# A bidirectional recurrence with a sign-weight product: eight products moved to earlier steps, the last row groups in another order

## The chip, the cores and the metric

One core of one Trainium2 chip runs the whole program. The metric is device time in microseconds of one execution; three runs of the kernel before gave 488.4, 488.56 and 490.11 us, a median of 488.56. One further execution was taken by the hardware profiler.

## The reference, cut to what matters

With B = 4 batches, T = 1024 positions and C = 1024 channels:

```
decay = exp(-exp(w)) * (0.5 + 0.5 * tf)           # per batch and channel
ek, ekv = exp(k), exp(k) * k                       # k is also v
nf, nb = scan of ekv over t, forward and backward  # a = a * decay + ekv_t
df, db = scan of ek  over t, forward and backward
num = nf + nb - ekv + exp(u + k) * k
den = df + db - ek  + exp(u + k)
y = sigmoid(x) * num / max(den, 1e-8) * (0.8 + 0.2 * tf)
bw = sign(weight) * mean(|weight|) per output row
out = x + y @ bw.T + bias
```

## The kernel before

The recurrence runs over 32 blocks of 128 channels, block g = 8 * batch + cc, each a tile of 128 channels by 1024 positions. The loop `for g in range(steps)` makes one step for each; all engines' orders are written out by hand in it (`tc.manual_schedule()`), so an instruction waits behind whatever stands ahead of it on its engine.

In one step TensorE turns the rows of k for block g + 1 into `kT` (L272, `pe_transpose_k`) and the rows of sigmoid(x) for block g into `sgT` (L278, `pe_transpose_gate`). There is one buffer of each in PSUM: `kT` may be written again when VectorE has made `euk` from it (L362), and `sgT` when VectorE has read it in `dve_newton_gate` (L429). VectorE runs the four scans (L372 forward, L385 backward; the backward ones start from a value that ScalarE makes, L378, `edge_num` and `edge_den`) and three or four further operations. ScalarE makes the exponentials (L284, L290), the logarithm (L410) and the reciprocal (L417), and casts the finished block to a high part (L439, `act_hi`); GpSimd multiplies and makes the low part (L444, `lo_part`). So each finished block stands in `gated` as two parts, and each product with a block is two matmuls.

The product with the signs of the weight is spread over later steps. For the first three batches it comes in groups q of 128 output channels by 512 positions, 16 groups a batch: `pe_product` (L455) adds eight blocks into a PSUM tile of the pool `ps_o`, which has three buffers; `act_scale` (L467) scales it to `z`; `pe_turn` (L475) turns `z` back to rows; `act_leave` (L565) copies it to a staged tile, and every second group is stored. `parts[g][0..4]` lists what step g issues at its five places: place 0 ahead of `kT`, place 1 behind it, place 2 ahead of `sgT`, places 3 and 4 behind it. In the kernel before, groups 37 to 47 (the last eleven of the third batch) fill places of four blocks each from step 26 on, and end with places 0 and 1 of step 30. The queues `fresh`, `ready`, `scaled` and `leaving` hold groups that are done, can be scaled, can be turned, and can leave.

The last batch has its product the other way round, with rows of positions as the output: row groups n = 0 to 7 of 128 positions, in two halves (part 0 and 1) of 512 columns, 16 matmuls each (`pe_wide_product`, L523). Rows 6 (`begun`) have five of eight blocks done early as `partial` tiles (`pe_partial`, in step 30), which ScalarE copies out (L560). Some of the wide tiles are begun in steps 30 and 31 with the blocks that are ready. The tiles of rows 3 take the buffer of `sgT`; so that it is free, ScalarE copies the gate of the last block to `gate_of_last` (L821). Behind the loop, VectorE finishes block 31 in two halves, TensorE adds blocks 30 and 31 to rows 0 to 3, and then makes rows 4, 5, 7 and the rest of rows 6. VectorE scales each half by `alpha_rows` (L540), adds it to rows of x + bias (L542), and SP stores the rows (L839, `store_rows`).

Of the kernel before, what the change touches and what calls it, by code (L numbers as in the profile page):

```python
# [9 lines left out]
F32 = mybir.dt.float32  # L10
# [11 lines left out]
def kernel(  # L22
# [27 lines left out]
    nc = tc.nc  # L50
    P = 128
    B, T, C = x.shape
    TD = time_emb.shape[1]
    NT = T // P
    NC = C // P
# [13 lines left out]
    num_pool = ctx.enter_context(tc.tile_pool(name="num_pool", bufs=3))  # L69
# [4 lines left out]
    ps_o = ctx.enter_context(tc.tile_pool(name="ps_o", bufs=3, space=bass.MemoryType.PSUM))  # L74
# [6 lines left out]
    sg_ps = {}  # L81
# [437 lines left out]
    def pe_wide_columns(t, n, cols, blocks, ends=(0, NC - 1)):  # L519
        h, s = divmod(n, PER)  # L520
        for cc in blocks:
            for i in range(2):
                nc.tensor.matmul(  # L523
                    t,
                    gated[last, cc, h][:, i, s * P : (s + 1) * P],
                    wT[:, cc, cols],
                    start=(cc == ends[0] and i == 0),
                    stop=(cc == ends[1] and i == 1),
                )
# [6 lines left out]
    def columns(part):  # L536
        return slice(part * H, (part + 1) * H)

    def leave_columns(ps, n, cols):
        nc.vector.tensor_mul(ps, ps, alpha_rows[:, cols])  # L540
        xs = x_rows[n][:, cols]
        nc.vector.tensor_add(xs, xs, ps)  # L542
# [5 lines left out]
    begun = NT - 2  # L548
# [3 lines left out]
    def pe_partial(part):  # L552
        t = ps_o.tile([P, H], F32, tag="po", name=f"partial_{part}")
        pe_wide_columns(t, begun, columns(part), range(NC - 3), (0, NC - 4))
        partial_ps[part] = t
# [13 lines left out]
    steps = B * NC  # L569
# [6 lines left out]
    parts = {g: [[] for _ in range(5)] for g in range(steps)}  # L576
    late = {g: [] for g in range(steps)}
    groups = NH * NC

    def pieces(qs):  # L580
        return [(q, part) for q in qs for part in (front, back)]

    def fill(g, part, items):
        for i, piece in enumerate(items):
            ahead, at = divmod(part + i, 5)
            parts[g + ahead][at].append(piece)

    for g in range(lag, 2 * NC + 1):
        q = 2 * (g - lag)
# [13 lines left out]
        late[g + 1].append((q + i, range(NC - 1, NC)))  # L603
    for part, piece in enumerate(pieces((q + 3, q + 4))):
        parts[g + 1][1 + part].append(piece)
    fill(g + 2, 0, pieces(range(q + 5, q + groups)))


    adds = {g: [] for g in range(steps + 1)}
# [15 lines left out]
    g = 3 * NC  # L625
# [3 lines left out]
    with tc.manual_schedule():  # L629
# [39 lines left out]
        def done():  # L669
            while fresh:  # L670
                ready.append(fresh.pop(0))

        def scale():
            while ready:
                scaled.append(ready.pop(0))
                act_scale(scaled[-1])
# [6 lines left out]
        def leave():  # L683
            if leaving:
                act_leave(leaving.pop(0))

        for g in range(steps):
            b, cc = divmod(g, NC)
            final = g == steps - 1
            if g + 2 < steps:  # L690
                load_k(g + 2)
                for i in gate_loads[g]:
                    load_gate(i)
            else:
                load_x_rows(g + 2 - steps, rows, "k_rows")
                load_x_rows(g + 4 - steps, gate_rows, "sg_rows")
            if g < NC:
                load_weight(g)
            if g in begins:
                begin_rows(begins[g])  # L700
            if final:
                alpha_rows = load_along_rows(den_pool, "den", "alpha_rows", alpha_dram)

            if g > 0:
                dve_denominator(g - 1)
                dma_own_numerator(g - 1)
            for i in adds[g]:
                add_x(*i)
            if final:
                done()  # L710
            scale()
            if final:
                act_partial(1)
            done()
            if g > 1:
                act_hi(g - 2, 0)
                act_hi(g - 2, 1)
            product(parts[g][0])
            if final:
                pe_wide_product(1, 1, range(NC - 3))  # L720
                pe_wide_product(2, 0, range(NC - 3))
            turn()
            if g > 0:
                floor_den(g - 1)
            if g > 0 and not adds[g]:
                act_log(g - 1)
            pool_clamp(g)
            if g > 1:
                lo_part(g - 2, 0)
                lo_part(g - 2, 1)  # L730
            product(late[g][:2])
            if late[g]:
                done()
            if g > 0:
                forward(g, nums[g])
            act_edge(g, nums[g], "edge_num")
            if g > 0 and adds[g]:
                act_log(g - 1)
            if g > 0:
                act_reciprocal(g - 1)  # L740
                den_product(g - 1)
            if g > 0:
                dve_own_terms(g)
            scale()
            done()
            leave()
            if 1 <= g <= NC:
                prepare_weight(g - 1)
            if g == NC:
                out_scales()  # L750
            if not final:
                pe_transpose_k(g + 1)
                product(late[g][2:])
                act_exponentials(g + 1)
                act_own_exponentials(g + 1)
            scale()
            product(parts[g][1])
            turn()
            if final:
                for i in ((1, 0), (1, 1), (2, 0)):  # L760
                    pe_wide_product(*i, range(NC - 3, NC - 2))
                pe_wide_product(0, 0, range(NC - 2))
            backward(g, nums[g], "edge_num")
            if final:
                dma_own_numerator(g)
            if g > 0:
                num_product(g - 1)
            forward(g, dens[g])
            act_edge(g, dens[g], "edge_den")
            leave()  # L770
            done()
            scale()
            product(parts[g][2])
            if g == steps - 2:
                pe_partial(0)
            if g > 0:
                dve_newton_gate(g - 1)
            if g > 0 and not final:
                gated_product(g - 1)
            for i in gates[g]:  # L780
                act_gate(i)
            if gates[g]:
                log_exp_tables()
            pe_transpose_gate(g)
            if g == 3 * NC - 1:
                load_gate(g + 4)
            product(parts[g][3])
            turn()
            if g == steps - 2:
                leave()  # L790
                act_partial(0)
                pe_partial(1)
            if parts[g][4]:
                done()
            product(parts[g][4])
            if g == steps - 2:
                pe_wide_product(1, 0, range(NC - 3))
            leave()
            backward(g, dens[g], "edge_den")
            if not final:  # L800
                dve_numerator_terms(g + 1)
            if g == NC:
                store_alpha()
# [6 lines left out]
        for i in adds[steps]:  # L810
            add_x(*i)

        for ts in halves:
            dve_denominator(g, ts)
        for ts in halves:
# [1 line left out]
            act_log(g, ts)  # L817
        for ts in halves:
            act_reciprocal(g, ts)
        gate = num_pool.tile([P, T], F32, tag="num", name="gate_of_last")  # L820
        nc.scalar.copy(gate, sg_ps[g])  # L821
        sg_ps[g] = gate
        for i in ((0, 1), (2, 1), (3, 0), (3, 1)):
            pe_wide_product(*i, range(NC - 2))
        gated_product(g - 1, engine=nc.vector)
# [12 lines left out]
        def store_rows(n, cols=slice(0, C)):  # L838
            nc.sync.dma_start(  # L839
                out=out[last, n * P : (n + 1) * P, cols], in_=x_rows[n][:, cols]  # L840
            )
# [4 lines left out]
        for n, part in waiting:  # L846
            leave_wide(n, part)
            if part == 1:
                store_rows(n)
        for n, part in ((4, 0), (4, 1), (5, 0), (5, 1), (7, 0), (7, 1)):  # L850
            pe_wide_product(n, part, range(NC))

            for i in ((0, 1) if part else ()) if n == 5 else (part,):
                leave_wide(n, i)
            if (n, part) == (4, 1):
                nc.vector.tensor_mul(partials[0], partials[0], alpha_rows)
                nc.vector.tensor_add(x_rows[begun], x_rows[begun], partials[0])
            if part == 1 and n != 7:
                store_rows(n)
        store_rows(7)  # L860
        for cols in (slice(0, H), slice(H, 3 * H // 2), slice(3 * H // 2, C)):
            t = ps_o.tile([P, cols.stop - cols.start], F32, tag="po", name=f"rest_{cols.start}")
            pe_wide_columns(t, begun, cols, range(NC - 3, NC), (NC - 3, NC - 1))
            leave_columns(t, begun, cols)
            store_rows(begun, cols)


# [28 lines left out]
```

## Time and profile before

| what | value |
|---|---|
| median of three runs | 488.56 us (488.4 to 490.11) |
| the profiled execution's own time | 488.17 us |
| span of its instructions | 486.4 us |
| mean granted TensorE clock | 0.906 |
| busy: PE, DVE, ACT, POOL | 364.9, 468.9, 337.4, 406.2 us |
| first start of kT of block 31 on PE | 416.97 us |
| last VectorE instruction, start | 482.82 us |

The profile names TensorE PE (its weight loads PEld), VectorE DVE, ScalarE ACT, GpSimd POOL and SyncE SP. Times are microseconds from the span's start. A line of a timeline reads: start, length, engine, line of the kernel, operation, output and inputs, shape, count, and in brackets how long the engine stood idle before it and what ended that. The ends of matmuls are modelled; with pipelining, one may be issued before the modelled end of the last. PEclk is the granted clock as a share of full speed.

### The profile page before, as it was taken

What the parts mean: (1) busy time and instruction counts of PE and PEld (TensorE: products, weight loads), DVE (VectorE), ACT (ScalarE), POOL (GpSimd) and SP (SyncE); (2) the same over time, 40 slices, a digit from 0 to 9 for tenths busy, and PEclk for the clock granted to TensorE, in tenths of its full rate; (3) what the DMA queues carried; (4) which work ended last, traced back from release to release, by engine and by line L of the source; (5) the groups of instructions that cost most, each with busy time, mean ns of one, the idle gap of its engine ahead of it and who ended that gap; (6) DMA issues with size and microseconds to landing.
All of it is one profiled execution on the core that took longest, in us unless ns stands there. A gap on an engine that the chain in (4) does not pass through costs nothing.

```text
span 486.4 us, 5204 instructions
## 1 busy us (share of the span) xinstructions
PE 364.9 (75%) x1803; PEld 297.1 (61%) x1803; DVE 468.9 (96%) x325; ACT 337.4 (69%) x468; POOL 406.2 (84%) x280
## 2 busy tenths in 40 slices
PE   3444433344588777778899898965999998999996
PEld 2333332333466665566677777754887777888884
DVE  6999999999999999999999999999999999999864
ACT  4795968859576968859697968877867979734000
POOL 3379999999999999999999999999999999983000
PEclk9995566666699999999999999995999999999999
DMA  8877569896399595969877996979649797899963
GB/s 230 245 217 185 160 171 222 171 263 166 92 261 218 141 223 145 226 166 235 197 185 163 261 225 170 204 177 237 153 77 275 168 236 240 172 279 268 226 222 130
DMA packets 91282, 97.35 MB, mean 200 GB/s; under 512 B 2772, under 2 KB 80888, under 8 KB 89208
## 3 DMA queue, kind: packets, MB, share of 16 engines
q1 hardware_dynamic: 84264, 63.45, 44.0%
q0 software_dynamic: 6976, 33.57, 36.1%
q8 instruction: 14, 0.23, 0.2%
q14 instruction: 12, 0.10, 0.1%
q10 hardware_dynamic: 16, 0.00, 0.0%
HBM read 63.46 MB, written 37.75 MB: 208 GB/s over the span
## 4 chain that ended last, share of the span: by engine, by line
DVE 76%; PE 17%; issue 3%; ACT 3%; DMA 0%; SPq 0%; DVEq 0%; ACTq 0%
DVE den L385 13%; DVE num L385 13%; DVE num L372 13%; DVE den L372 12%; PE wide L523 9%; DVE den L395 7%; DVE num L356 6%; DVE den L429 6%; DVE euk L362 3%; PE po L455 3%; PE partial L523 1%; PE wide_t L523 1%; PE bank L523 1%; PE sgT L278 1%; PE kT L272 1%
## 5 line engine op out<-in xcount | busy, mean ns | idle before, releaser
L455 PE MATMUL po<-gated,wT 128*128 128x512 f32 x768 | 199.8, 408 | 0.3 <-ACT staged L565 0.3
L455 PEld LDWEIGHTS po<-gated,wT 128*128 128x128 f32 x768 | 142.0, 192 | 30.4 <-ACT staged L565 0.8
L272 PE MATMUL kT<-ident,k_rows 128*128 128x128 f32 x248 | 43.0, 330 | 61.8 <-issue 42.9
L444 POOL TENSOR_TENSOR gated<-num,gated 128x512 fp32r<-128x512 f32 x60 | 75.8, 1282 | 2.4
L278 PE MATMUL sgT<-ident,sg_rows 128*128 128x128 f32 x256 | 43.1, 323 | 45.5 <-DVE den L429 36.4
L272 PEld LDWEIGHTS kT<-ident,k_rows 128*128 128x128 f32 x248 | 34.6, 170 | 69.8 <-issue 51.8
L385 DVE TENSOR_TENSOR_SCAN den<-bank,edge_den,den 128x1024 f32<-128x1024 f32 x32 | 74.9, 2342 | 0.6 <-ACT edge_den L378 0.4
L422 POOL TENSOR_TENSOR den<-den,eu 128x1024 f32<-128x1024 f32 x31 | 73.8, 2379 | 1.4 <-ACT eu L417 1.4
L385 DVE TENSOR_TENSOR_SCAN num<-bank,edge_num,num 128x1024 f32<-128x1024 f32 x32 | 74.9, 2340 | 0.0
L434 POOL TENSOR_TENSOR num<-den,num 128x1024 f32<-128x1024 f32 x30 | 71.9, 2395 | 2.8 <-DVE den L429 0.5
L425 POOL TENSOR_TENSOR num<-num,eu 128x1024 f32<-128x1024 f32 x31 | 73.5, 2372 | 0.7 <-DMA num<-euk 0.7
L372 DVE TENSOR_TENSOR_SCAN den<-bank,den 128x1024 f32<-128x1024 f32 x32 | 72.3, 2260 | 0.0
L372 DVE TENSOR_TENSOR_SCAN num<-bank,num 128x1024 f32<-128x1024 f32 x31 | 70.6, 2279 | 0.0
L278 PEld LDWEIGHTS sgT<-ident,sg_rows 128*128 128x128 f32 x256 | 35.1, 166 | 56.4 <-DVE den L429 29.6
L439 ACT CAST gated<-num 128x512 fp32r<-128x512 f32 x64 | 36.5, 619 | 28.4 <-POOL num L434 24.6
L410 ACT ACTIVATE eu<-den,gain 128x1024 f32<-128x1024 f32 (+1 forms) x33 | 36.8, 1119 | 22.8 <-POOL den L402 17.8
L402 POOL TENSOR_SCALAR den<-den,floor 128x1024 f32<-128x1024 f32 x31 | 37.8, 1219 | 17.2 <-DVE den L395 13.8
L523 PE MATMUL wide<-wT,gated 128*128 128x512 f32 x192 | 45.1, 392 | 0.0
L565 ACT COPY staged<-turned 128x512 f32<-128x512 f32 x48 | 27.5, 574 | 21.2 <-PE turned L475 21.2
L395 DVE SCALAR_TENSOR_TENSOR den<-eu,top,den 128x1024 f32<-128x1024 f32 (+1 forms) x33 | 41.7, 1267 | 0.0
L523 PEld LDWEIGHTS wide<-wT,gated 128*128 128x128 f32 x192 | 35.9, 188 | 8.2 <-ACT gate_of_last L821 0.4
L362 DVE SCALAR_TENSOR_TENSOR euk<-eu,top,kT 128x1024 f32<-128x1024 f32 x31 | 38.8, 1252 | 0.0
(98 smaller groups left out, 577.9 us busy)
## 6 DMA issues: line engine op xcount, KB each, us to landing
sg_rows<-in_x_dram SPq DMA_DIRECT2D x32, 512.0 KB, 6.2
num<-euk POOLq DMA_DIRECT2D x32, 512.0 KB, 5.9
out_dram<-in_x_dram POOLq DMA_DIRECT2D x16, 1024.0 KB, 11.7
k_rows<-in_fside_BxSxS_dram SPq DMA_DIRECT2D x31, 512.0 KB, 5.1
out_dram<-staged SPq DMA_DIRECT2D x24, 512.0 KB, 5.6
w_rows<-in_L_ffn_weight_dram SPq DMA_DIRECT2D x8, 512.0 KB, 7.2
out_dram<-in_L_ffn_bias_dram SPq DMA_DIRECT2D x4, 1024.0 KB, 10.1
x_rows<-out_dram SPq DMA_DIRECT2D x8, 512.0 KB, 5.5
```

The costliest lines, as they stand in the source:

```text
L272: nc.tensor.transpose(kT[:, s * P : (s + 1) * P], k_rows[g][:, s, :], ident)
L278: nc.tensor.transpose(t[:, s * P : (s + 1) * P], sg_rows[g][:, s, :], ident)
L362: nc.vector.scalar_tensor_tensor(euk, eus[g], top[:, b, cc : cc + 1], k_ps[g], ALU.min, ALU.mult)
L372: nc.vector.tensor_tensor_scan(t, decay_row(g), t, 0.0, ALU.mult, ALU.add)
L385: nc.vector.tensor_tensor_scan(back, decay_row(g), back, inits[g, which], ALU.mult, ALU.add)
L395: nc.vector.scalar_tensor_tensor(dens[g][:, ts], eus[g][:, ts], top[:, b, cc : cc + 1], dens[g][:, ts], ALU.min, ALU.add,)
L422: engine.tensor_mul(dens[g][:, ts], dens[g][:, ts], eus[g][:, ts])
L425: engine.tensor_mul(nums[g][:, ts], nums[g][:, ts], eus[g][:, ts])
L434: engine.tensor_mul(nums[g][:, ts], dens[g][:, ts], nums[g][:, ts])
L444: engine.tensor_sub(t[:, 1, :], nums[g][:, h * H : (h + 1) * H], t[:, 0, :].bitcast(F32))
L455: nc.tensor.matmul(prods[q], wT[:, cc, oc * P : (oc + 1) * P], gated[b, cc, h][:, i, :], start=(cc == 0 and i == 0), stop=(cc == NC - 1 an ...
L523: nc.tensor.matmul(t, gated[last, cc, h][:, i, s * P : (s + 1) * P], wT[:, cc, cols], start=(cc == ends[0] and i == 0), stop=(cc == ends[1 ...
```

## The change

Groups 37 to 47 are cut into other portions: at steps 28 and 29 place 0 gets six blocks in place of four, so that step 30 has only place 0. At steps 29 and 30 a second `scale()` stands ahead of the exponentials. `pe_partial(1)` follows `pe_partial(0)` at once, ahead of `sgT`. The copy `gate_of_last` moves ahead of the last block's logarithms. The row groups behind the loop end with rows 7 in place of rows 6: the rest of rows 6 comes in two halves behind rows 5, and rows 7 in a half and two quarters.

```diff
--- before.py
+++ after.py
@@ -603,7 +603,16 @@
         late[g + 1].append((q + i, range(NC - 1, NC)))
     for part, piece in enumerate(pieces((q + 3, q + 4))):
         parts[g + 1][1 + part].append(piece)
-    fill(g + 2, 0, pieces(range(q + 5, q + groups)))
+
+    blocks = [(i, cc) for i in range(q + 5, q + groups) for cc in range(NC)]
+    sizes = [4] * 5 + [4] * 5 + [6, 4, 4, 4, 4] * 2 + [4]
+    for i, n in enumerate(sizes):
+        ahead, at = divmod(i, 5)
+        for j, cc in blocks[sum(sizes[:i]) : sum(sizes[: i + 1])]:
+            items = parts[g + 2 + ahead][at]
+            if not items or items[-1][0] != j:
+                items.append((j, []))
+            items[-1][1].append(cc)
 
 
     adds = {g: [] for g in range(steps + 1)}
@@ -743,6 +752,8 @@
                 dve_own_terms(g)
             scale()
             done()
+            if steps - 4 < g < steps - 1:
+                scale()
             leave()
             if 1 <= g <= NC:
                 prepare_weight(g - 1)
@@ -773,6 +784,7 @@
             product(parts[g][2])
             if g == steps - 2:
                 pe_partial(0)
+                pe_partial(1)
             if g > 0:
                 dve_newton_gate(g - 1)
             if g > 0 and not final:
@@ -789,7 +801,6 @@
             if g == steps - 2:
                 leave()
                 act_partial(0)
-                pe_partial(1)
             if parts[g][4]:
                 done()
             product(parts[g][4])
@@ -810,6 +821,10 @@
         for i in adds[steps]:
             add_x(*i)
 
+        gate = num_pool.tile([P, T], F32, tag="num", name="gate_of_last")
+        nc.scalar.copy(gate, sg_ps[g])
+        sg_ps[g] = gate
+
         for ts in halves:
             dve_denominator(g, ts)
         for ts in halves:
@@ -817,9 +832,6 @@
             act_log(g, ts)
         for ts in halves:
             act_reciprocal(g, ts)
-        gate = num_pool.tile([P, T], F32, tag="num", name="gate_of_last")
-        nc.scalar.copy(gate, sg_ps[g])
-        sg_ps[g] = gate
         for i in ((0, 1), (2, 1), (3, 0), (3, 1)):
             pe_wide_product(*i, range(NC - 2))
         gated_product(g - 1, engine=nc.vector)
@@ -847,7 +859,7 @@
             leave_wide(n, part)
             if part == 1:
                 store_rows(n)
-        for n, part in ((4, 0), (4, 1), (5, 0), (5, 1), (7, 0), (7, 1)):
+        for n, part in ((4, 0), (4, 1), (5, 0), (5, 1)):
             pe_wide_product(n, part, range(NC))
 
             for i in ((0, 1) if part else ()) if n == 5 else (part,):
@@ -855,14 +867,20 @@
             if (n, part) == (4, 1):
                 nc.vector.tensor_mul(partials[0], partials[0], alpha_rows)
                 nc.vector.tensor_add(x_rows[begun], x_rows[begun], partials[0])
-            if part == 1 and n != 7:
+            if part == 1:
                 store_rows(n)
-        store_rows(7)
+
+        def finish(n, cols, blocks):
+            t = ps_o.tile([P, cols.stop - cols.start], F32, tag="po", name=f"rest_{n}_{cols.start}")
+            pe_wide_columns(t, n, cols, blocks, (blocks[0], NC - 1))
+            leave_columns(t, n, cols)
+
+        for part in range(2):
+            finish(begun, columns(part), range(NC - 3, NC))
+        store_rows(begun)
         for cols in (slice(0, H), slice(H, 3 * H // 2), slice(3 * H // 2, C)):
-            t = ps_o.tile([P, cols.stop - cols.start], F32, tag="po", name=f"rest_{cols.start}")
-            pe_wide_columns(t, begun, cols, range(NC - 3, NC), (NC - 3, NC - 1))
-            leave_columns(t, begun, cols)
-            store_rows(begun, cols)
+            finish(7, cols, range(NC))
+            store_rows(7, cols)
 
 
 # ---- launch: one core; inputs and outputs as the reference has them ----
```

## The prediction

> **What bounds the kernel now.** I read the page first (busy time, clock), then the chain of waits, then the timelines of TensorE, VectorE and ScalarE around its last turn, then the clock by windows.
>
> From the page, busy time:
>
> ```profile
> PE 364.9 (75%) x1803; PEld 297.1 (61%) x1803; DVE 468.9 (96%) x325; ACT 337.4 (69%) x468; POOL 406.2 (84%) x280
> ```
>
> VectorE is busy 96% of the span and carries the chain as far as block 30. The chain of waits (start, length, what) shows where that ends:
>
> ```profile
> 415.74 1.19 DVE euk L362
> ...
> 416.97 1.09 PE kT L272 x8
> 418.06 1.87 PE po L455 x8
> ...
> 426.39 4.58 PE wide L523 x20
> ...
> 437.38 0.87 PE sgT L278 x8
> ...
> 455.00 23.82 PE wide L523 x104
> ...
> 478.85 0.71 DVE wide L540
> ...
> 482.82 0.42 DVE x_rows L542
> ```
>
> From 416.97 to 478.83 TensorE works without a gap, so each matmul removed there is time, until another wait ends later. Before that TensorE pauses, which costs nothing by itself. Its timeline:
>
> ```profile
> 389.87 1.09 PE L272 MATMUL kT<-ident,k_rows 128*128 128x128 f32 x8 [0.36 <-DVE euk L362]
> ...
> 395.46 1.09 PE L278 MATMUL sgT<-ident,sg_rows 128*128 128x128 f32 x8 [0.31 <-DVE den L429]
> ...
> 403.48 1.09 PE L272 MATMUL kT<-ident,k_rows 128*128 128x128 f32 x8 [0.45 <-DVE euk L362]
> ...
> 407.36 0.66 PE L475 MATMUL turned<-ident,z 128*128 128x128 f32 x4 [0.92 <-ACT z L467]
> ```
>
> The bracket counts from the modelled end of the matmul before. What could be issued there is larger: a matmul of 512 columns costs 0.229 us (23.82 / 104) and four transposes 0.44 us, so the gap before kT of block 29 is 389.87 - (388.91 + 0.44) = 0.52, before the gate of block 28 it is 395.46 - (393.03 + 1.83) = 0.60, before kT of block 30 it is 403.48 - (402.43 + 0.44) = 0.61, before the turn at 407.36 it is 407.36 - (404.33 + 1.83) = 1.20.
>
> **Part 1, the eight products.** By the built order, steps 28 and 29 each issue four more matmuls (two channel blocks, two parts each) ahead of kT, and the eight behind kT of block 31 are gone. Four cost 0.92. Step 28: 0.92 - 0.52 puts kT 0.40 late (390.27); ScalarE reads it only at 392.23, and the 0.60 before the gate absorbs it. Step 29: 0.92 - 0.61 = 0.31 late (403.79). There the added scale() moves z ahead of the exponentials, so the turn that waited no longer does: 403.79 + 0.85 + 1.83 + 0.44 + 1.83 = 408.74, then the wait for VectorE's L429 (407.79 + 1.19 = 408.98). The gate starts near 409.04, not 409.73, with all eight done. What follows (0.87 + 1.83 + 0.44 + 3.67 + 0.44) ends at 416.29; kT of block 31 still waits for L362 and starts at 416.97. So the pauses hide the eight entirely, and the gain can only appear behind 416.97.
>
> **Part 2, behind kT of block 31.** Before, eight matmuls 1.87, turn 0.44, partial 2.31, gate 0.96, turn 0.44, partial 2.31 lead from 418.06 to 426.39. Now one turn, two partials and the gate remain, but that turn needs the scaled last group, and this z is late on ScalarE. Its timeline of before:
>
> ```profile
> 413.31 0.78 ACT L467 ACTIVATE z<-po,wub,out_scale 128x512 f32<-128x512 f32 x1
> ...
> 415.78 0.30 ACT L378 ACTIVATE edge_num<-num,edge 128x1 f32<-128x1 f32 x1 [0.66 <-DVE num L372]
> ...
> 418.20 0.76 ACT L467 ACTIVATE z<-po,wub,out_scale 128x512 f32<-128x512 f32 x1
> ```
>
> A z now stands ahead of the table loads at 408.69 (0.68 from start to start), so their end moves from 413.31 to 413.99. Then come a copy (0.47), a z (0.68) and two casts (1.13): edge_num starts at 416.27, 0.49 later. The logarithm and the reciprocal follow as before, and z of the last group runs from 418.69 to 419.45. TensorE stands from 418.06 to 419.46, then 0.44 + 4.62 + 0.87 brings the wide products to 425.4: **0.98 us gained, not 1.83**. Both ends: were ScalarE on time, z would end at 418.96 and the gain be 1.45; were it 0.3 later still, 0.68. I take 0.98, since each term is a row.
>
> **Part 3, how far the gain carries.** The next wait is the gate of block 31, which needs VectorE's L429 on the tile it overwrites (VectorE's timeline):
>
> ```profile
> 434.89 1.19 DVE L429 SCALAR_TENSOR_TENSOR den<-den,sgT 128x1024 f32<-128x1024 f32 x1
> ```
>
> It ends at 436.08, so TensorE, at 437.38 before, cannot gain over 1.28 here; at 436.40 it passes. The pair of wide products of rows 3 then needs the copy of that gate, in ScalarE's timeline:
>
> ```profile
> 442.70 0.99 ACT L821 COPY gate_of_last<-sgT 128x1024 f32<-128x1024 f32 x1
> ```
>
> At its old place the copy ended at 443.69 and the pair started at 443.76, so an earlier TensorE would have lost all it had gained. Moved ahead of the logarithm, the copy runs from about 437.3 to 438.3, while ScalarE waits for VectorE anyway (idle from 435.30 to 440.23), and it also removes VectorE's 0.22 wait at 443.73. The bank tile is free at 438.35, wanted at 440.0; the last two blocks' parts are ready at 446.4, wanted near 448.3; the leaving products move with TensorE. The first partial's copy no longer waits 1.23 for a store. All this costs nothing.
>
> **Part 4, the order of the last groups.** Before, after 478.83 VectorE still had the last product of rows 7 and three pieces of rows 6: 483.24 - 478.83 = 4.41, while TensorE did 18 matmuls beside it and started its last at 481.3. Now rows 6 go first and rows 7 end in two pieces of 256 columns. Twenty matmuls of 256 columns replace ten of 512: the rows of rest give (481.3 - 480.02) / 11 = 0.116 each, so 20 x 0.116 - 10 x 0.229 = +0.03. Upper bound: if each waited for a weight load of 0.188 (the rest row), 20 x 0.188 - 2.29 = +1.47; the twelve in the trace kept 0.116, so I take 0.03. The last matmul ends at 481.3 + 0.276 + 0.03 = 481.6 without part 1, and one small piece follows (0.46 + 0.42): 482.55 against 483.24, a gain of 0.70. The last store stays 128 KB and lands in the 1.9 us of before.
>
> Sum: 0.98 + 0.70 = 1.7. The profiled execution (488.17, 1.77 around its span of 486.4) would become 486.5; it stands 0.39 below the median of 488.56, so against that the forecast is **486.9**.
>
> **Rivals.** (a) Slower: the clock halves in the new pause. PE by windows of 3.41 us (busy, count, granted clock):
>
> ```profile
> 211.09:214.50 3.41, 1.60 (x13) 1.00 1.01 212
> ...
> 323.73:327.14 3.41, 0.66 (x4) 1.00 1.11 297
> 327.15:330.56 3.41, 1.97 (x8) 0.50 0.60 195
> ```
>
> A window with 0.66 busy was followed by half clock for 13.65 us; one with 1.60 was not. From 416.29 the new order has 0.68 idle, kT 1.09, 1.40 idle: the worst window holds some 1.3, between the two and nearer the second. It decides below some value from 0.66 to 1.6. Half clock for 10.24 us (the usual stretch in the first 130 us) costs 5.1: 488.56 + 5.1 - 1.7 = 492.0. Chance 0.06. The Trainium skill ("TensorE: Matmul & The Clock Gate", Part 1 with Part 4) says that an idle window of about 3.4 us brings the half clock and that transposes do not count as busy in the same way. By that the new pause, with kT alone in it, would be close to idle; but here the window from 43.84 to 47.25 held 3.38 us of transposes alone and the clock rose to 1.00 behind it, so the trace disagrees and the chance stays small.
>
> (b) VectorE is held by the later ScalarE. edge_num would end at 416.56, wanted at 416.84; edge_den at about 422.0, wanted at 422.41. If both miss by 0.8 more than this slack, L429 of block 30 ends at about 437.7, the gain of part 1 is lost and 0.3 more: 488.56 + 0.3 - 0.7 = 488.2. Tail alone: 487.9. For it: slack of only 0.3 to 0.4; against: every term is a row. Chance 0.12.
>
> (c) More is won: ScalarE on time (capped at 1.28), and the last store lands sooner, as less is queued ahead of it (1 MB was issued in the last 5 us, now half). No landing below 1.9 is seen; bounded by the 3.16 between VectorE's end and the span's, I give it 0.5: 488.56 - 1.28 - 0.70 - 0.5 = 486.1, or lower if these runs fall like the profiled one. Chance 0.24.
>
> (d) A slip in the order that I cannot price, of several us, slower: 0.05.
>
> **How the numbers follow.** About 0.5%, 2.4 us, is what a measurement of this kernel can tell from no change: faster is below 486.1, slower above 491.0. The forecast (gains of 1.3 to 2.0) has 0.53. (a) and (d) are slower, 0.11; (c) is faster in most of its cases, and the scatter of runs (488.4 to 490.11) adds a little: 0.25; the rest, 0.64, is within. The range, from 485.8 (c with scatter) to 488.9 (tail alone with scatter), leaves out (a), (d) and little else.
>
> **What would show it.** Right: no kT or gate pause over 0.3 at steps 28 and 29; a wait of some 1.4 on z ahead of the last turn; the gate of block 31 starting near 436.4; VectorE ending about 1.7 earlier, behind two pieces of 256 columns. Wrong: VectorE waiting for edge_num or edge_den near 417 or 422, half clock behind 417, or matmuls of 256 columns spaced well over 0.116.

## The result and the profile after

The changed kernel took 486.55 us (median of five runs, 486.34 to 487.42) against 488.4 for the kernel before, measured beside it (five runs, 488.28 to 490.11): a ratio of 0.9963 with a 95% interval of 0.9952 to 0.9974. That is 1.85 us faster, under 0.5%; the forecast was 486.9. Its profiled execution took 486.48, with a span of 484.7.

The chain of waits of the changed kernel (start, length, what), for the same stretch as before:

```profile
418.64 0.77 ACT z L467
...
419.46 0.66 PE turned L475 x4
420.12 4.59 PE partial L523 x20
...
425.58 4.59 PE wide L523 x20
...
436.60 0.87 PE sgT L278 x8
...
442.98 9.15 PE wide L523 x40
...
470.44 10.19 PE rest L523 x60
...
481.12 0.42 DVE x_rows L542
```

The chain no longer runs through kT of block 31 but through ScalarE: TensorE stands until z of the last group ends, and from 419.46 to 480.63 it works without a gap. The wide products start at 425.58 where they started at 426.39, the gate of block 31 at 436.60 for 437.38, the 40 matmuls that begin with rows 3 take 9.15 where they took 9.41, and VectorE's last addition starts at 481.12 for 482.82.

The timeline of TensorE in the changed kernel, at the places shown of before:

```profile
390.31 1.04 PE L272 MATMUL kT<-ident,k_rows 128*128 128x128 f32 x8
...
395.50 1.09 PE L278 MATMUL sgT<-ident,sg_rows 128*128 128x128 f32 x8
...
403.85 1.04 PE L272 MATMUL kT<-ident,k_rows 128*128 128x128 f32 x8
...
409.07 1.09 PE L278 MATMUL sgT<-ident,sg_rows 128*128 128x128 f32 x8
...
417.02 1.09 PE L272 MATMUL kT<-ident,k_rows 128*128 128x128 f32 x8 [0.37 <-DVE euk L362]
419.46 0.66 PE L475 MATMUL turned<-ident,z 128*128 128x128 f32 x4 [1.35 <-ACT z L467]
```

The four brackets of before are gone: the pauses are filled. The two that remain are the wait for L362, where nothing can be won as VectorE carries the chain up to there, and a new one of 1.35 for z.

### The profile page after: what moved, and what is told of

Its sections match the earlier page's. It is cut to its first block, busy times and chain, and to the rows that moved or that the text cites. A ratio compares the mean times of both kernels' runs of the same rounds, so it can differ in the third digit from the quotient of the medians.

```text
span 484.7 us, 5221 instructions
## 1 busy us (share of the span) xinstructions
PE 362.5 (75%) x1813; PEld 295.3 (61%) x1813; DVE 468.9 (97%) x325; ACT 337.8 (70%) x468; POOL 406.7 (84%) x280
## 4 chain that ended last, share of the span: by engine, by line
DVE 69%; PE 20%; ACT 5%; issue 5%; DMA 0%; SPq 0%; DVEq 0%; ACTq 0%
DVE num L385 13%; DVE den L385 12%; DVE den L372 12%; DVE num L372 11%; PE wide L523 8%; DVE den L395 6%; DVE num L356 6%; DVE den L429 6%; PE po L455 5%; DVE euk L362 3%; PE rest L523 2%; PE sgT L278 1%; PE partial L523 1%; PE kT L272 1%; PE bank L523 1%
## 5 line engine op out<-in xcount | busy, mean ns | idle before, releaser
L272 PE MATMUL kT<-ident,k_rows 128*128 128x128 f32 x248 | 41.5, 322 | 61.1 <-issue 42.8
L272 PEld LDWEIGHTS kT<-ident,k_rows 128*128 128x128 f32 x248 | 33.4, 165 | 68.8 <-issue 51.8
L362 DVE SCALAR_TENSOR_TENSOR euk<-eu,top,kT 128x1024 f32<-128x1024 f32 x31 | 38.9, 1256 | 0.0
L523 PE MATMUL wide<-wT,gated 128*128 128x512 f32 x160 | 37.8, 393 | 0.0
L467 ACT ACTIVATE z<-po,wub,out_scale 128x512 f32<-128x512 f32 x48 | 37.2, 776 | 0.8 <-PE po L455 0.7
```

The lines of the kernel that those rows point to most:

```text
L272: nc.tensor.transpose(kT[:, s * P : (s + 1) * P], k_rows[g][:, s, :], ident)
L362: nc.vector.scalar_tensor_tensor(euk, eus[g], top[:, b, cc : cc + 1], k_ps[g], ALU.min, ALU.mult)
L523: nc.tensor.matmul(t, gated[last, cc, h][:, i, s * P : (s + 1) * P], wT[:, cc, cols], start=(cc == ends[0] and i == 0), stop=(cc == ends[1 ...
```

## The experiments

The theory is the prediction's: two gains in different places. One lies on TensorE behind kT of block 31, cut to under 1 us by the wait for z, and kept only by the earlier copy of the gate; the other is the order of the last groups. The first rival says that the whole gain is that order. Times are medians; where a few tenths of a microsecond matter, the profiles are read instead. The kernel before was measured anew beside each set of runs: 488.18 beside the first four, 488.12 beside the last three, 488.4 beside the changed kernel. So gains against it compare better than times do.

**The copy of the gate back in its old place.**

```diff
-        gate = num_pool.tile([P, T], F32, tag="num", name="gate_of_last")
-        nc.scalar.copy(gate, sg_ps[g])
-        sg_ps[g] = gate
...
         for ts in halves:
             act_reciprocal(g, ts)
+        gate = num_pool.tile([P, T], F32, tag="num", name="gate_of_last")
+        nc.scalar.copy(gate, sg_ps[g])
+        sg_ps[g] = gate
```

> The changed kernel with the copy of the last gate back behind the reciprocals. Main theory (two gains, one on TensorE ahead of the gate of block 31, one in the order of the last groups; the first survives only because the copy was moved): TensorE reaches rows 3 near 443.0 as in the changed kernel, waits for the copy until about 443.8, and the part gained ahead of it is lost; VectorE waits again about 0.2. Span near 485.75, time 487.4 to 487.8, that is 0.9 to 1.1 slower than the changed kernel. Rival (the whole gain is the order of the last groups, the copy only shifts idle time of ScalarE): 486.5, span 484.7, as the changed kernel.

Measured: 487.47, ratio 0.9985 (0.9976 to 0.9994), span 485.7. TensorE's timeline of this run at rows 3:

```profile
439.97 2.91 PE L523 MATMUL bank<-wT,gated 128*128 128x512 f32 x12
443.70 9.43 PE L523 MATMUL wide<-wT,gated 128*128 128x512 f32 x40 [0.82 <-ACT gate_of_last L832]
```

TensorE was ahead, and lost it all at this one copy: the pair of rows 3 starts at 443.70, where it started at 443.76 before. What is left of the gain is that of the last groups. The 40 matmuls behind the wait again take 9.43 and not 9.15.

**The old order of the last groups.** The code behind rows 5 is that of the kernel before; all else is as changed.

```diff
-        for n, part in ((4, 0), (4, 1), (5, 0), (5, 1)):
+        for n, part in ((4, 0), (4, 1), (5, 0), (5, 1), (7, 0), (7, 1)):
...
-        for part in range(2):
-            finish(begun, columns(part), range(NC - 3, NC))
-        store_rows(begun)
+        store_rows(7)
         for cols in (slice(0, H), slice(H, 3 * H // 2), slice(3 * H // 2, C)):
-            finish(7, cols, range(NC))
-            store_rows(7, cols)
+            t = ps_o.tile([P, cols.stop - cols.start], F32, tag="po", name=f"rest_{cols.start}")
+            pe_wide_columns(t, begun, cols, range(NC - 3, NC), (NC - 3, NC - 1))
+            leave_columns(t, begun, cols)
+            store_rows(begun, cols)
```

> The changed kernel with the last row groups in the old order (rows 7, then the rest of rows 6). Main theory: about 0.65 of the gain goes, VectorE has some 4.4 of work behind the last product of rows 7 again; time 487.1 to 487.3, span near 485.35. Rival (the whole gain is this order): 488.2 to 488.4, as the kernel before.

Measured: 486.99, span 485.2; the ratio of 0.9982 (0.9973 to 0.9991) contains two of the eleven runs that took 488.6, for which no cause is on record. Its chain ends:

```profile
453.80 23.82 PE wide L523 x104
...
481.61 0.42 DVE x_rows L542
```

The last wide product ends at 477.61 and VectorE's last addition at 482.03, so 4.4 of VectorE's work stands behind TensorE again. The first gain is there without the second: 1.2 of span.

**The new order of the last groups alone**, on the kernel before (the edit above the other way round).

> The kernel before with the new order of the last row groups alone. Main theory: 0.65 gained, time 487.6 to 487.8, span near 485.75; TensorE's steps up to 454 unchanged. Rival (the whole gain is this order): 486.5.

Measured: 487.45, ratio 0.9984 (0.9976 to 0.9993), span 485.8. Its chain, from rows 3 on to TensorE's last matmul:

```profile
455.08 16.48 PE wide L523 x72
471.56 10.19 PE rest L523 x60
```

It wins 0.6 of span, with TensorE as late as before up to 455. The two gains add up, in spans 1.2 + 0.6 against 1.7, in medians against the kernel before 1.19 + 0.73 against 1.85. The rival that the order is the whole gain has fallen.

**Without the added scale().**

```diff
-            if steps - 4 < g < steps - 1:
-                scale()
```

> The changed kernel without the added second scale() of steps 29 and 30. Main theory (the wait for z ahead of the last turn is the price of the moved products, and the added scale() holds it down): z of the last group runs behind the two exponentials, near 421.2 instead of 418.6, the last turn starts near 422 instead of 419.5, and nothing later absorbs it; about 2.4 slower than the changed kernel: 488.6 to 489.2, no faster than the kernel before. Rival (the turn has slack, because the two partials could be done in any case): 486.5 to 486.8.

Measured: 491.38, ratio 1.0063 (1.0051 to 1.0076), span 488.8: slower, and by over 2 more than expected. TensorE's timeline, and PE by windows of 3.41 us (busy, count, granted clock) of this run:

```profile
422.21 0.69 PE L475 MATMUL turned<-ident,z 128*128 128x128 f32 x4 [3.67 <-ACT z L467]
422.62 6.43 PE L523 MATMUL partial<-wT,gated 128*128 128x512 f32 x20
```

```profile
419.28:422.69 3.41, 0.48 (x5) 1.00 1.11 203
422.69:426.10 3.41, 3.41 (x10) 0.50 0.94 351
```

The turn is 2.75 later than in the changed kernel, near the expectation. Then the clock halves for one window, and the twenty matmuls of the partials take 6.15 in this run's chain for 4.59: 1.56 more. 2.75 + 1.56 = 4.3 is the lateness of the wide products (429.92 for 425.58), and 4.2 reaches the end. The profiled execution is the fastest of its five (490.63); what made the median another 0.75 longer is not shown. So the prediction's rival of the halved clock is real. It came here behind a pause of 3.67, where the change made one of 1.35, and it was smaller than its price: one window and 1.56, not three windows (10.24) and 5.1. In the changed kernel, by the same view:

```profile
417.58:420.99 3.41, 2.06 (x14) 1.00 1.04 197
```

**The first partial product ahead of the last turn.**

```diff
             product(parts[g][1])
+            if g == steps - 2:
+                pe_partial(0)
             turn()
...
             if g == steps - 2:
-                pe_partial(0)
                 pe_partial(1)
```

> The changed kernel with the first partial product of rows 6 ahead of the last turn, so that TensorE works while ScalarE makes z. Main theory (the pause of 1.35 ahead of the last turn is the last of the slack, and behind it the gate of block 31 can't start ahead of VectorE's L429, which ends at 436.15): the pause is gone, the gate starts near 436.2 instead of 436.6, and only 0.4 to 0.5 is gained: 486.0 to 486.1, span near 484.3, with a new wait for L429 ahead of that gate. Rival (TensorE's work behind block 31 is the whole bound, the gate's tile is no limit): 1.4 gained, 485.1.

Measured: 486.2, span 484.3. TensorE's timeline of this run:

```profile
417.76 2.56 PE L523 MATMUL partial<-wT,gated 128*128 128x512 f32 x10
420.16 0.60 PE L475 MATMUL turned<-ident,z 128*128 128x128 f32 x4
...
426.54 2.56 PE L523 MATMUL wide<-wT,gated 128*128 128x512 f32 x10 [0.29 <-ACT partial L560]
...
436.16 1.09 PE L278 MATMUL sgT<-ident,sg_rows 128*128 128x128 f32 x8 [0.65 <-DVE den L429]
```

The pause is gone and the wait for L429 takes its place, where the prediction had put the limit. TensorE was 1.65 ahead at the gate of block 30 (422.90 for 424.55), and of this 0.22 is left behind the gate of block 31 (437.25 for 437.47 in the chains). The span is 0.4 shorter; another 0.14 of that is the last 60 matmuls, which took 10.05 for 10.19 though no edit touched them. The runs do not tell this kernel from the changed one: the ratio is 0.9960 (0.9948 to 0.9973) for 0.9963.

**And the second product of rows 0 ahead of the gate of block 31.** In addition to the edit before:

```diff
                 pe_wide_product(0, 0, range(NC - 2))
+                pe_wide_product(0, 1, range(NC - 2))
...
-        for i in ((0, 1), (2, 1), (3, 0), (3, 1)):
+        for i in ((2, 1), (3, 0), (3, 1)):
```

> As the run before, and the second product of rows 0 ahead of the gate of block 31, which gives TensorE 2.75 of work before it needs L429. Main theory: no wait at the gate; but the copy of the first partial waits for a store that lands near 426.2, and the second product of rows 1 needs its tile near 426.3, so about 0.5 is lost there: 1.0 gained against the changed kernel, 485.5, span near 483.7. Rival (the copy has slack): 1.5 gained, 485.0.

Measured: 485.51 (485.06 to 485.93), ratio 0.9947 (0.9933 to 0.9960). The median is the one expected. The profiled run is the fastest, 485.06 with a span of 483.3, and near the rival's 485.0; in it the store landed earlier, the partials' copy began at 425.53, and TensorE lost some 0.25 at rows 1 (20 matmuls in 4.83 for 4.58). The gate starts at 437.87 without a wait.

**And another tile for the partial.** In addition:

```diff
-            partials.append(resid.tile([P, C], F32, tag="x_res", name="partial"))
+            partials.append(eu_pool.tile([P, C], F32, tag="eu", name="partial"))
```

> As the run before, with the partial copied to a free tile of another pool, so that it needn't wait for the store. Main theory: the copy starts near 423.7 and 1.5 is gained against the changed kernel: 485.0, span near 483.2. Rival (another wait takes its place: the tile of rows 4, which VectorE frees near 454.3, or the low part of block 29 near 431): 485.4 to 485.6.

Measured: 485.19 (485.06 to 485.53), ratio 0.9940 (0.9928 to 0.9952), span 483.3. TensorE and ScalarE of this run, and what TensorE's weight loads (PEld) waited for:

```profile
430.58 1.38 PE L523 MATMUL wide<-wT,gated 128*128 128x512 f32 x4
```

```profile
423.56 1.08 ACT L560 COPY partial<-partial 128x512 f32<-128x512 f32 x2 [1.27 <-POOL num L425]
```

```profile
PEld wide L523 <- POOL gated L444: 0.4, 1, 0.4
...
PEld wide L523 <- DVE x_rows L542: 0.3, 1, 0.3
```

The copy starts at 423.56 as expected, but both waits that the rival had named take its place. The four matmuls at 430.58 take 1.38 for 1.08, as their weight load waits 0.4 for the low part of block 29; and the load for rows 4 waits 0.3 until VectorE frees the tile at 454.2, so that the 72 matmuls there take 16.64 for 16.48. The span is 1.4 shorter than that of the changed kernel, 0.14 of it again in the last 60 matmuls; against the kernel before measured beside each, the gains are 2.93 and 1.85. The median is the lowest of all versions, but the best run and the span are those of the run before, and the intervals overlap: that the other tile won anything is not shown.

## Why the prediction was right

**Part 1** held to 0.1: kT at 390.31 and 403.85 (forecast 390.27 and 403.79), the gate of block 28 at 395.50, hardly later than its 395.46 of before, that of block 29 at 409.07 (409.04), kT of block 31 at 417.02 (416.97). The pauses hid the eight products.

**Part 2** was right in its mechanism: z started at 418.64 (418.69), the turn at 419.46 (419.46). The size of the gain was 0.81, not 0.98: the mis-sized term is the turn, taken at 0.44 from a stream without a gap. Behind a wait it costs 0.66 in the chain. The row at 407.36 of before, with its 0.66, had shown it. The 1.83 that the prediction sets against its 0.98 is not what a TensorE without the wait would gain: a turn moved along with the eight matmuls, and 0.44 + 4.62 + 0.87 = 5.93 in place of 8.33 would be 2.40 earlier. The forecast does not rest on that figure.

**Part 3**: 0.78 was left at the gate of block 31, which started at 436.60 and not 436.40, clear of L429. The copy of the gate ran from 437.56. Two things were wrong. The prediction took the old copy as just in time, at no cost to the kernel before. In fact the pair of rows 3 already paid for it there: its 40 matmuls took 9.41, against 9.15 now, as a weight load had waited for the copy. From the chain and the waits of the kernel before:

```profile
443.76 9.41 PE wide L523 x40
```

```profile
PEld wide L523 <- ACT gate_of_last L821: 0.4, 1, 0.4
```

The experiments agree: 9.43 in the two with the copy at its old place (the late gate, the order alone), 9.15 to 9.16 in the others. So the earlier copy is worth 0.26 by itself, which the sum lacked. And the partial's copy was to wait no more for a store; it waited longer:

```profile
426.24 1.08 ACT L560 COPY partial<-partial 128x512 f32<-128x512 f32 x2 [3.77 <-DMA out_dram<-staged]
```

It ended by 427.3, and the second product of rows 1 needed the first half's tile near 427.87, so it cost nothing here. Had TensorE been some 1 us faster there it would have: the sixth experiment's expectation came from this, and the wait of 0.29 at 426.54 in the fifth shows it.

**Part 4**: 0.65 for 0.70. The 32 matmuls of 256 columns took 10.19 - 28 x 0.229 = 3.78, or 0.118 each for 0.116; the bound of 0.188 did not come.

The sum: 0.78 + 0.26 + 0.65 = 1.69, against 486.4 - 484.7 = 1.7 of span. (The 1.2 of the run with the old order stands 0.16 above 0.78 + 0.26 because z of its last group began 0.16 earlier, at 418.48.) The mechanism was as forecast; that the sum met to 0.01 is luck: 0.20 too much up to the gate and 0.05 too much in part 4 met 0.26 that was missing. The runs isolate the copy, the added scale() and the order of the last groups; the new portions and the place of the second partial product were not tried one by one.

**The rivals.** The halved clock did not come: the window with the pause held 2.06 us of work in this execution, more than the 1.3 of the worst case. Wherever a window falls there, it holds at least 1.69, over the 1.60 of the window that kept the full clock in the kernel before. The half clock came in the run without the added scale(), at 0.48. VectorE was not held: edge_num ended at 416.51, wanted at 416.88, edge_den at 421.99, wanted at 422.48. Nothing more was won either: ScalarE was as late as forecast, and the last store took its 1.9 as before.

## What to carry to other kernels

When work is moved into an engine's pauses, the gain is set by what the engine meets where the work was: here the wait for z behind kT, then the gate's tile, then the copy that frees it. Follow the engine forward, wait by wait, with the rows' numbers, and price the first instruction behind a wait from a row that also waited. Work that needs nothing new (the partial product) fills the pause when it stands ahead of the instruction that waits for another engine. By itself this won no time that the runs can tell here, since the next limit stood close behind; with that limit removed too, the gain against the kernel before grew from 1.85 to over 2.6. Each limit removed shows the next one, in the order that the trace gives.

## What the runs showed of the hardware

- Work right behind a wait took TensorE 0.2 to 0.3 longer in the chains: four transposes 0.66 for 0.44, forty matmuls 9.41 to 9.43 for 9.15. That held also in the kernel before, where no idle time was shown ahead of the forty matmuls and only a weight load had waited, 0.4.
- One window of 3.41 us with 0.48 of work halved the clock for the next window and cost 1.56, in the midst of otherwise full work; a window with 2.06 did not. In the kernel before, a window with 0.66 was followed by four windows at half clock, which held 1.97, 0.00, 1.64 and 3.41 of work; here the first window at half clock was full, and it stayed the only one. The Trainium skill ("TensorE: Matmul & The Clock Gate", Part 1) says that an idle window of about 3.4 us brings the half clock; the trace agrees, with the addition that the window need not be wholly idle.
- A store of 512 KB issued 4.8 us earlier did not land earlier. Before, it was issued at 419.46 and took 6.4; in the changed kernel it was issued at 414.64 and took 11.5, so it landed near 426 in both. Two loads of rows that were issued at 404.8 before, well ahead of it, are issued at 415.2 now, right behind it; whether they, or the 1 MB that GpSimd's queue was adding at the time, held it back was not tried.
